# Latent attention beside local attention on one core: the second halves of the queries and keys issued at the end of a step, and the side work dealt out anew over the 36 steps

## The chip, the cores and the metric

One Trainium2 chip, one of its cores. The metric is the device time of one launch in microseconds (us), median of several runs. Times of single instructions come from one profiled execution.

## The reference, cut to what matters

The input x has 8 batches of 1024 rows of 256 numbers, all float32. Two blocks follow each other, each with a layer normalisation ahead of it and a residual sum behind it. The change touches the first one alone, latent attention with a shared rotary part:

```python
c_kv = x @ W_kv_down                                   # 256 -> 128
k_rope = rotary(c_kv @ W_k_rope)                       # 32 wide, one for all heads
k, v = c_kv @ W_k_up, c_kv @ W_v_up                    # 16 heads of 16
q, q_rope = x @ W_q, rotary(x @ W_q_rope)
scores = (q . k per head + q_rope . k_rope) / sqrt(48) # causal
x = x + softmax(scores) @ v @ W_o
```

The second block (two layers of windowed attention with a gated MLP) follows on all batches, and is the same before and after.

## The kernel before, in words

The first block is the function `mla` (lines 156 to 650), the second one `local` (from line 658). In `mla` the attention of one batch is cut into 36 units, one a step (`units`, lines 597 to 603). Steps 0 to 25 treat query columns 512 to 1023 (c = 1), first heads 0 to 7 (g = 0 and 1, steps 0 to 12), then heads 8 to 15 (g = 2 and 3, steps 13 to 25). Steps 26 to 35 treat query columns 0 to 511 (c = 0) in the same two parts. The exponential of a score is a product of two: exp of the head's own part, and `er`, exp of the rotary part, which all heads share.

In step s the main loop (lines 613 to 646) writes out, in this order:

- `scores` of unit s (line 444): 8 score products on TensorE (line 455) into two tiles of two PSUM banks each, pool `pscore`, two such tiles in all; then two exponentials on ScalarE (line 463), one a tile, into `pt` (6 buffers).
- the entries "low" of the step (line 624).
- `turned` of unit s-1 (line 467): two products pt times er on VectorE (line 477).
- `values` of unit s-2 (line 479): the products with v on TensorE (line 488); where a head group ends, ScalarE copies the sum (`oaT`, line 496).
- `do(b, step)` (line 638): the other entries of the step.
- `turn_back` and `finished` for head groups that ended one or two steps earlier (lines 500 to 521): on VectorE a transposition, a reciprocal and a product each, then a transposition for every second group, and after the last one a range test of the reciprocals (lines 1794, 1795, 1788).

All this stands in a manual schedule (line 613), so TensorE, VectorE, ScalarE and GpSimd each run their instructions in the order in which they are written.

The side work of a step is a table (lines 544 to 581) of tuples: the step, whose batch it is (-1 the one before, 0 this one, 1 the next, 2 the one after that), a name, its arguments. The names:

- `statistics(n, part)` (line 268): mean and variance of two row tiles on VectorE; with part 1 the power -1/2 and the shift on GpSimd follow (lines 285 to 288).
- `normalise(n, part)` (line 291): before, two row tiles a call on ScalarE (line 299).
- `turn(n, c)` (line 304): four transpositions on TensorE into one bank, copied by ScalarE to `xnT`.
- `down`, `rope_q`, `rope_k`, `query`, `keys`, `value` (lines 323 to 401): projections, through `dense` (line 313), which may be split over two steps; four column quarters of one product are four matmuls (line 201). `rope_q` and `rope_k` are followed by a VectorE product with the rotary tables (lines 335 and 342), the others by a ScalarE copy.
- `query` and `keys` end in `halves` (line 348): ScalarE copies the sum, rounded to fp32r, into the tile `halves` (two buffers). `low` (line 353) then subtracts that copy from the sum in PSUM by one matmul with minus the identity (line 355), copies the rest as the second half (line 356), and the four transfers of `place_q` or `place_k` (lines 370 and 385) are issued on SyncE.
- `rotary(c, kb)` (line 414): the rotary scores of one key block on TensorE, exp on ScalarE into `er` (line 418), on diagonal blocks a mask on GpSimd (line 420).
- `squares` and `reach` (lines 427 to 437): squares of the rotary parts on ScalarE, sums on TensorE, a maximum on VectorE (a range test).
- `out_add(t, i, c)` (line 523): the product with W_o on TensorE, the residual sum on VectorE (line 534), and the store to `x2d` on SyncE (line 535).
- `load`: the next x, on SyncE.

All of them take a PSUM bank from a pool of two (`psum1`), which is free again when the copy or sum has read it. From step `ALONE` on (line 610: one past the last step in which batch 0 of the table has work other than out_add, 16 before) the last batch gives these two banks to a third pair of score banks (lines 616 to 619). Two passes over the table ahead of the main loop (lines 605 to 608) prepare the first batch.

Of the kernel before, what the change touches and what calls it, by code (L numbers as in the profile page):

```python
# [31 lines left out]
AF = mybir.ActivationFunctionType  # L32
# [50 lines left out]
def preln_mla_local_kernel(  # L83
# [27 lines left out]
    nc = tc.nc  # L111
    B = x.shape[0]
# [43 lines left out]
    def mla(ctx: ExitStack, verdict):  # L156
# [101 lines left out]
        class Batch:  # L258
# [32 lines left out]
            def normalise(self, n, part):  # L291
# [5 lines left out]
                xn = self.xn[n]  # L297
                for i in (2 * part, 2 * part + 1):
                    nc.scalar.activation(
                        xn[:, i, :], self.x[:, 4 * n + i, :], AF.Identity, scale=rstd[:, i : i + 1],  # L300
                        bias=shift[:, i : i + 1],
                    )
# [241 lines left out]
        for step, who, *what in (  # L544
            (0, -1, "out_add", 6, 1, 1), (0, 0, "query", 1, 1, 0),
            (1, 0, "query", 1, 1, 1),
            (2, 0, "low"), (2, 0, "value", 2),
            (3, 0, "keys", 1, 0), (3, 1, "statistics", 1, 1),
            (4, 0, "low"), (4, 0, "keys", 1, 1), (4, 1, "normalise", 0, 0),
            (5, 0, "low"), (5, 0, "query", 0, 0, 0), (5, 1, "normalise", 0, 1),  # L550
            (6, 0, "query", 0, 0, 1), (6, 1, "normalise", 1, 0),
            (7, 0, "low"), (7, -1, "out_add", 0, 0), (7, -1, "out_add", 0, 1),
            (8, -1, "out_add", 2, 0), (8, -1, "out_add", 2, 1),
            (9, 0, "value", 3),
            (10, 0, "query", 1, 0, 0), (10, 1, "normalise", 1, 1),
            (11, 0, "query", 1, 0, 1), (11, 1, "turn", 0, 0),
            (12, 0, "low"), (12, 0, "rotary", 0, 0), (12, 1, "turn", 0, 1),
            (13, 0, "rotary", 0, 2), (13, 1, "down", 0, 0),
            (14, 0, "rotary", 0, 3), (14, 1, "down", 0, 1),
            (15, 0, "rotary", 0, 1), (15, 1, "turn", 1, 0),  # L560
            (16, 1, "down", 1, 0), (16, 1, "turn", 1, 1),
            (17, 1, "down", 1, 1), (17, 1, "rope_q", 0, 0, 0),
            (18, 1, "rope_q", 0, 0, 1), (18, 1, "rope_q", 0, 1),
            (19, 1, "rope_q", 1, 0), (19, 1, "rope_k", 0, 0),
            (20, 1, "rope_k", 0, 1), (20, 1, "rope_q", 1, 1), (20, 2, "load"),
            (21, 1, "rope_k", 1), (21, 1, "query", 0, 1, 0, 0),
# [30 lines left out]
        units = []  # L597
# [15 lines left out]
        with tc.manual_schedule(engines={E.PE, E.DVE, E.Activation, E.Pool}):  # L613
            for b in range(B + 1):
                for step in range(len(units) if b < B else 9):
# [23 lines left out]
                    if turning:  # L639
                        bt, e = turning.pop(0)  # L640
                        bt.turn_back(*e)
# [1250 lines left out]
```

## Time and profile before

| | |
|---|---|
| median of 3 runs | 3263.04 us (3262.31 to 3263.51) |
| the profiled execution | 3258.18 us |
| its span, first to last instruction | 3256.5 us |
| granted TensorE clock | 0.994 |
| busy over the span | PE 97%, DVE 81%, ACT 53%, POOL 41% |
| first exponential of the main loop | at 50.37 us |
| first exponential of batches 1 to 7 | 161.43, 275.25, 389.28, 504.01, 618.03, 731.86, 845.62 us |
| so one batch takes | 111.06 (batch 0), then 113.83, 114.03, 114.73, 114.02, 113.83, 113.77 us |

The last exponential of `mla` starts at 945.96 us; the rest of the span, some 2300 us, is the second block. PE is TensorE's matmuls, PEld its weight loads, DVE is VectorE, ACT ScalarE, POOL GpSimd, SP SyncE. Names are those of the program's tiles: sc are scores, pt their exponentials, acc the products with v, psq, psk, psv, psrq, psrk, psR, psc, psn and psx the banks of query, keys, value, rope_q, rope_k, rotary, down, turn and out_add. "place_q(1, 1)" in a name marks the `halves` tile of query m = 1, n = 1.

### The profile page before, as it was taken

The numbers are of one execution on the slowest core, as the hardware profiler recorded it, in microseconds if no ns is written. First come the engines' busy times: TensorE is split into PE (matmuls) and PEld (weight loads), VectorE is DVE, ScalarE is ACT, GpSimd is POOL, SyncE is SP. The second block draws the span as 40 slices with busy tenths as digits, with TensorE's granted clock in tenths as the row PEclk, the third lists the DMA queues.
The fourth block names the chain that finished last, engine by engine and source line by source line (L and its number), as shares of the span: only waits on it lengthen the run. The fifth ranks groups of instructions, "written<-read, shape, count | busy, mean of one in ns | idle before, by whom it ended". The sixth has DMA issues, their size and how long they took to land.

```text
span 3256.5 us, 112852 instructions
## 1 busy us (share of the span) xinstructions
PE 3161.7 (97%) x50274; PEld 1461.0 (45%) x50274; DVE 2650.2 (81%) x3934; ACT 1733.9 (53%) x2183; POOL 1344.1 (41%) x1065
## 2 busy tenths in 40 slices
PE   7999999999987999999999999999999999999998
PEld 2434343443433444444444444445444444444454
DVE  4999999999988788887878877777787878787773
ACT  6888888888852344444444444444444444444441
POOL 1001000000008665565555555555555555555540
PEclk9999999999998999999999999999999999999999
DMA  4133233323333444544444455455545545454431
GB/s 129 44 92 88 53 79 79 76 59 78 83 122 94 114 126 117 137 118 125 126 117 132 120 145 141 125 128 145 138 131 138 131 125 134 132 146 125 117 107 56
DMA packets 389902, 364.22 MB, mean 112 GB/s; under 512 B 158703, under 2 KB 337310, under 8 KB 389278
## 3 DMA queue, kind: packets, MB, share of 16 engines
q1 hardware_dynamic: 387422, 354.51, 40.8%
q8 instruction: 396, 6.49, 0.8%
q10 hardware_dynamic: 1984, 2.41, 0.2%
q14 instruction: 100, 0.82, 0.1%
HBM read 165.96 MB, written 140.51 MB: 94 GB/s over the span
## 4 chain that ended last, share of the span: by engine, by line
PE 84%; DVE 8%; ACT 3%; DMA 2%; issue 1%; SPq 1%; POOL 1%; ACTq 0%; DVEq 0%; POOLq 0%
PE ag L670 18%; PE pair L670 12%; PE psy L670 9%; PE psw L670 7%; PE acc L488 6%; PE pv L670 6%; PE o L1003 6%; PE sc L455 5%; PE pair L962 4%; DVE pt L477 4%; PE s L1011 2%; PE psx L201 1%; PE psR L201 1%; ACT pt L463 1%; PE psq L201 1%
## 5 line engine op out<-in xcount | busy, mean ns | idle before, releaser
L477 DVE TENSOR_TENSOR pt<-pt,er 128x1024 f32<-128x1024 f32 x576 | 671.7, 1220 | 35.2 <-ACT pt L463 35.1
L670 PE MATMUL ag<-d,l 128*32 128x512 f32 x5632 | 640.2, 593 | 1.2 <-DVE xs L1043 0.7
L906 POOL TENSOR_TENSOR t<-t,t 128x1024 f32<-128x1024 f32 x128 | 304.3, 2377 | 796.8 <-DVE t L902 796.8
L463 ACT ACTIVATE pt<-sc 128x1024 f32<-128x1024 f32 x576 | 561.1, 1033 | 115.1 <-PE sc L455 105.1
L968 ACT ACTIVATE pt<-pair 128x1024 f32<-128x1024 f32 (+1 forms) x256 | 235.2, 968 | 537.0 <-PE pair L962 496.4
L670 PE MATMUL pair<-l_qkv,xT 128*32 128x512 f32 x4096 | 468.6, 598 | 3.2 <-DMA xT<-zx 2.5
L126 POOL TENSOR_TENSOR rn<-ss,half 128x16 f32<-128x16 f32 x128 | 373.0, 2914 | 13.9
L488 PE MATMUL acc<-pt,v 128*32 128x512 f32 (+3 forms) x3072 | 344.8, 495 | 11.6 <-DVE pt L477 10.4
L670 PEld LDWEIGHTS ag<-d,l 128*32 128x32 f32 x5632 | 177.8, 110 | 373.8 <-issue 354.3
L897 ACT ACTIVATE sq<-pair 128x1024 f32<-128x1024 f32 x128 | 131.2, 1025 | 349.2 <-issue 300.6
L670 PE MATMUL psy<-l,hid 128*32 128x256 f32 x5120 | 282.1, 379 | 0.0
L670 PEld LDWEIGHTS pair<-l_qkv,xT 128*32 128x32 f32 x4096 | 131.5, 111 | 303.5 <-issue 276.3
L899 DVE TENSOR_TENSOR t<-pair,l_cos 128x1024 f32<-128x1024 f32 x128 | 156.0, 1219 | 121.6 <-ACT sq L897 121.2
L455 PE MATMUL sc<-q,k 32*128 32x512 f32 (+3 forms) x3072 | 245.9, 380 | 4.0 <-ACT pt L463 3.0
L912 POOL TENSOR_TENSOR t<-t,rn 128x1024 f32<-128x1024 f32 x128 | 243.5, 1902 | 10.0
L1003 PEld LDWEIGHTS o<-pt,v 128*32 128x32 f32 x7680 | 215.1, 110 | 68.1 <-issue 51.8
L1135 DVE SCALAR_TENSOR_TENSOR hid<-ag,l_b,ge 128x512 f32<-128x512 f32 x160 | 116.7, 730 | 157.4 <-ACT ge L1134 88.0
L670 PE MATMUL pv<-l_qkv,xT 128*32 128x512 f32 x2048 | 243.7, 592 | 0.0
L420 POOL TENSOR_SCALAR_AFFINE_SELECT er<-er 128x128 f32<-128x128 f32 x64 | 39.0, 609 | 481.3 <-ACT er L418 481.3
L1003 PE MATMUL o<-pt,v 128*32 128x128 f32 x7680 | 234.5, 273 | 3.1 <-POOL pt L970 2.8
L1021 DVE RECIPROCAL rs<-s 128x256 f32<-128x256 f32 x128 | 223.1, 1743 | 15.8 <-PE s L1011 15.7
L670 PE MATMUL psw<-l_o,oT 128*32 128x256 f32 x4096 | 234.7, 381 | 0.7 <-DVE xs L1172 0.7
(326 smaller groups left out, 4589.9 us busy)
## 6 DMA issues: line engine op xcount, KB each, us to landing
z<-turned SPq DMA_DIRECT2D x512, 128.0 KB, 2.4
qkT<-z SPq DMA_DIRECT2D x128, 512.0 KB, 3.4
y<-xs SPq DMA_DIRECT2D x128, 128.0 KB, 3.0
h<-y SPq DMA_DIRECT2D x32, 512.0 KB, 4.6
zx<-turneds SPq DMA_DIRECT2D x120, 128.0 KB, 3.0
xT<-zx SPq DMA_DIRECT2D x240, 64.0 KB, 2.5
zh<-turnedh SPq DMA_DIRECT2D x120, 128.0 KB, 2.4
d<-zh SPq DMA_DIRECT2D x30, 512.0 KB, 3.2
```

Source lines behind the costliest of these rows:

```text
L126: nc.gpsimd.tensor_tensor(out_, in_, half[:, :n], ALU.pow)
L455: nc.tensor.matmul(two[n // 2][:, n % 2, lo : lo + w], k[rows], q[rows, h], start=(h == 1), stop=(h == 0),)
L463: nc.scalar.activation(pt, sc, AF.Exp, scale=SCALE)
L477: nc.vector.tensor_tensor(t, t, er.to_broadcast([P, 1024 // w, w]), ALU.mult)
L488: nc.tensor.matmul(self.acc[g][32 * n : 32 * n + 32, q0 - c * 512 :], self.v[:, kb, h * VW : h * VW + 32], pts[n // 2][:, n % 2, lo : lo + w],
L670: nc.tensor.matmul(out[four], w[:, four], rhs, start=start, stop=stop)
L899: nc.vector.tensor_tensor(t1, qk, A[:, i].unsqueeze(2).to_broadcast([P, 2, HEADS, DH]), ALU.mult)
L906: nc.gpsimd.tensor_tensor(t1, t1, t2, ALU.add)
L912: nc.gpsimd.tensor_tensor(t1, t1, rn.unsqueeze(3).to_broadcast([P, 2, HEADS, DH]), ALU.mult)
L968: nc.scalar.activation(pt[:, :, : n * P], flat[:, :, : n * P], AF.Exp, scale=-1.0)
L1003: nc.tensor.matmul(o[32 * j : 32 * j + 32, g, a, :], vs[m][:, h * DH + a * 32 : h * DH + a * 32 + 32], pts[m][g][:, place(j), off : off + ...
L1021: nc.vector.reciprocal(rs, s)
```

## The change

The table is laid out anew. Each "low" now stands in the step after the one that completes its product, as before, but is issued after the other entries of that step: `do(b, step, low=True)` moves from behind the scores to behind `do(b, step)`, and so behind the products with v. `normalise` treats one row tile a call, in eight steps (3 to 10) in place of two tiles in four (4, 5, 6 and 10). The two statistics of the upper rows move from steps 34 and 3 to 4 and 5, those of the lower rows from 23 and 26 to 24 and 25. `reach` goes from 32 to 30, an out_add from 31 and 32 to 31, two others from 7 and 8 to 6 and 10. keys(1, 1) goes from step 4 to 11; the rotary blocks of c = 0 from 12 to 15 to 13, 14, 16 and 17, which moves ALONE to 18. The one split rope_k and one split query become whole, one rope_q becomes split. After the last batch the loop runs over 11 steps in place of 9, for the later out_add. No product is added or left out.

```diff
--- before.py
+++ after.py
@@ -294,12 +294,10 @@
                     if n == 0:
                         self.xn = []
                     self.xn.append(p1.tile([P, 4, D], F32, tag="xn", name=f"xn{self.b}_{n}", bufs=2))
-                xn = self.xn[n]
-                for i in (2 * part, 2 * part + 1):
-                    nc.scalar.activation(
-                        xn[:, i, :], self.x[:, 4 * n + i, :], AF.Identity, scale=rstd[:, i : i + 1],
-                        bias=shift[:, i : i + 1],
-                    )
+                nc.scalar.activation(
+                    self.xn[n][:, part, :], self.x[:, 4 * n + part, :], AF.Identity, scale=rstd[:, part : part + 1],
+                    bias=shift[:, part : part + 1],
+                )
 
             def turn(self, n, c):
                 if n == c == 0:
@@ -544,39 +542,39 @@
         for step, who, *what in (
             (0, -1, "out_add", 6, 1, 1), (0, 0, "query", 1, 1, 0),
             (1, 0, "query", 1, 1, 1),
-            (2, 0, "low"), (2, 0, "value", 2),
-            (3, 0, "keys", 1, 0), (3, 1, "statistics", 1, 1),
-            (4, 0, "low"), (4, 0, "keys", 1, 1), (4, 1, "normalise", 0, 0),
-            (5, 0, "low"), (5, 0, "query", 0, 0, 0), (5, 1, "normalise", 0, 1),
-            (6, 0, "query", 0, 0, 1), (6, 1, "normalise", 1, 0),
-            (7, 0, "low"), (7, -1, "out_add", 0, 0), (7, -1, "out_add", 0, 1),
-            (8, -1, "out_add", 2, 0), (8, -1, "out_add", 2, 1),
-            (9, 0, "value", 3),
-            (10, 0, "query", 1, 0, 0), (10, 1, "normalise", 1, 1),
-            (11, 0, "query", 1, 0, 1), (11, 1, "turn", 0, 0),
-            (12, 0, "low"), (12, 0, "rotary", 0, 0), (12, 1, "turn", 0, 1),
-            (13, 0, "rotary", 0, 2), (13, 1, "down", 0, 0),
-            (14, 0, "rotary", 0, 3), (14, 1, "down", 0, 1),
-            (15, 0, "rotary", 0, 1), (15, 1, "turn", 1, 0),
-            (16, 1, "down", 1, 0), (16, 1, "turn", 1, 1),
-            (17, 1, "down", 1, 1), (17, 1, "rope_q", 0, 0, 0),
-            (18, 1, "rope_q", 0, 0, 1), (18, 1, "rope_q", 0, 1),
-            (19, 1, "rope_q", 1, 0), (19, 1, "rope_k", 0, 0),
-            (20, 1, "rope_k", 0, 1), (20, 1, "rope_q", 1, 1), (20, 2, "load"),
-            (21, 1, "rope_k", 1), (21, 1, "query", 0, 1, 0, 0),
-            (22, 1, "query", 0, 1, 0, 1), (22, 1, "query", 0, 1, 1), (22, 1, "squares", 0),
-            (23, 1, "low"), (23, 1, "keys", 0, 0), (23, 2, "statistics", 0, 0), (23, 1, "squares", 1),
-            (24, 1, "low"), (24, 1, "value", 0),
-            (25, 1, "value", 1),
-            (26, 1, "keys", 0, 1), (26, 2, "statistics", 0, 1),
-            (27, 1, "low"), (27, 1, "rotary", 1, 0),
-            (28, 1, "rotary", 1, 1),
-            (29, 1, "rotary", 1, 2), (29, 1, "rotary", 1, 7),
-            (30, 1, "rotary", 1, 3),
-            (31, 1, "rotary", 1, 6), (31, 0, "out_add", 4, 0),
-            (32, 0, "out_add", 4, 1), (32, 1, "reach"),
-            (33, 1, "rotary", 1, 4),
-            (34, 1, "rotary", 1, 5), (34, 2, "statistics", 1, 0),
+            (2, 0, "value", 2), (2, 0, "low"),
+            (3, 0, "keys", 1, 0), (3, 1, "normalise", 0, 0),
+            (4, 0, "query", 0, 0, 0), (4, 0, "low"), (4, 1, "normalise", 0, 1), (4, 1, "statistics", 1, 0),
+            (5, 0, "query", 0, 0, 1), (5, 1, "normalise", 0, 2), (5, 1, "statistics", 1, 1),
+            (6, -1, "out_add", 0, 0), (6, -1, "out_add", 0, 1), (6, 0, "low"), (6, 1, "normalise", 0, 3),
+            (7, 0, "query", 1, 0, 0), (7, 1, "normalise", 1, 0),
+            (8, 0, "query", 1, 0, 1), (8, 1, "normalise", 1, 1),
+            (9, 0, "value", 3), (9, 0, "low"), (9, 1, "normalise", 1, 2),
+            (10, -1, "out_add", 2, 0), (10, -1, "out_add", 2, 1), (10, 1, "normalise", 1, 3),
+            (11, 0, "keys", 1, 1),
+            (12, 1, "turn", 0, 0), (12, 0, "low"),
+            (13, 0, "rotary", 0, 2), (13, 1, "turn", 0, 1),
+            (14, 1, "down", 0, 0), (14, 0, "rotary", 0, 3),
+            (15, 1, "down", 0, 1), (15, 1, "turn", 1, 0),
+            (16, 0, "rotary", 0, 0), (16, 1, "turn", 1, 1),
+            (17, 1, "down", 1, 0), (17, 0, "rotary", 0, 1),
+            (18, 1, "down", 1, 1), (18, 1, "rope_q", 0, 0, 0),
+            (19, 1, "rope_q", 0, 0, 1), (19, 1, "rope_q", 0, 1),
+            (20, 1, "rope_k", 0), (20, 1, "rope_q", 1, 0, 0), (20, 2, "load"),
+            (21, 1, "rope_q", 1, 0, 1), (21, 1, "rope_q", 1, 1),
+            (22, 1, "rope_k", 1), (22, 1, "query", 0, 1, 0),
+            (23, 1, "query", 0, 1, 1), (23, 1, "squares", 0),
+            (24, 1, "value", 0), (24, 1, "low"), (24, 1, "squares", 1), (24, 2, "statistics", 0, 0),
+            (25, 1, "keys", 0, 0), (25, 2, "statistics", 0, 1),
+            (26, 1, "value", 1), (26, 1, "low"),
+            (27, 1, "keys", 0, 1), (27, 1, "rotary", 1, 7),
+            (28, 1, "rotary", 1, 0), (28, 1, "low"),
+            (29, 1, "rotary", 1, 1), (29, 1, "rotary", 1, 6),
+            (30, 1, "reach"),
+            (31, 0, "out_add", 4, 0), (31, 0, "out_add", 4, 1),
+            (32, 1, "rotary", 1, 3),
+            (33, 1, "rotary", 1, 2),
+            (34, 1, "rotary", 1, 4), (34, 1, "rotary", 1, 5),
             (35, 0, "out_add", 6, 0), (35, 0, "out_add", 6, 1, 0),
         ):
             at(step, who, *what)
@@ -612,7 +610,7 @@
         line, done, turning = [], [], []
         with tc.manual_schedule(engines={E.PE, E.DVE, E.Activation, E.Pool}):
             for b in range(B + 1):
-                for step in range(len(units) if b < B else 9):
+                for step in range(len(units) if b < B else 11):
                     if b == B - 1 and step == ALONE:
                         banks.close()
                         third = banks.enter_context(tc.tile_pool(name="pscore2", bufs=1, space=PSUM))
@@ -621,7 +619,6 @@
                         if step == 0:
                             batches[b].start()
                         line.append((batches[b], units[step], batches[b].scores(step, units[step])))
-                    do(b, step, low=True)
                     if len(line) > 1 or b == B:
                         for bt, unit, pts in line[-2 : -1] if b < B else line[-1:] if step == 0 else []:
                             bt.turned(unit, pts)
@@ -636,6 +633,7 @@
                         for act, args in held[2:]:
                             act(*args)
                     do(b, step)
+                    do(b, step, low=True)
                     if turning:
                         bt, e = turning.pop(0)
                         bt.turn_back(*e)
```

## The prediction

> **What bounds the kernel now.** I read the page first, then the steady batch from 275.25 to 389.28 us in four views: busy time by stage, the chain of waits, the timeline of TensorE, the groups by form on each engine.
>
> ```profile
> PE 3161.7 (97%) x50274; PEld 1461.0 (45%) x50274; DVE 2650.2 (81%) x3934; ACT 1733.9 (53%) x2183; POOL 1344.1 (41%) x1065
> ```
> ```profile
> 275.25:389.28 114.03, 111.31 (x1290) 45.65 (x1292) 105.66 (x131) 96.64 (x128) 9.62 (x14) 1.00 0.30 75
> ```
>
> In the stage that changes, the columns are PE, PEld, DVE, ACT and POOL busy: PE 111.3 of 114.0, DVE 105.7, ACT 96.6. Three engines are nearly full, so small local overloads decide. The chain shows an undisturbed step, and three kinds of disturbed ones:
>
> ```profile
> 335.46 0.66 PE sc L455 x5
> 336.13 1.00 PE acc L488 x8
> 337.13 0.86 PE psrq L201 x8
> 337.99 0.43 PE psrk L201 x8
> 338.42 0.67 PE sc L455 x6
> ...
> 284.22 0.47 SPq L370
> ...
> 286.05 5.09 DMA q<-alves_place_q(1, 1)_3282
> 291.23 0.59 ACT alves_place_k(1, 1)_3410 L79
> 291.87 0.49 PE psk L355
> ...
> 351.54 1.10 ACT sq L430
> 352.64 1.83 ACT pt L463 x2
> 354.52 0.79 PE sc L455 x12
> ...
> 382.44 0.63 DVE onat L504
> 383.10 0.26 DVE rs L506
> 383.38 0.42 DVE onat L510
> 383.81 2.38 DVE pt L477 x2
> 386.23 0.84 PE acc L488 x10
> ```
>
> The first five lines price a step on TensorE: scores 0.67, values 0.99, a 512-column product 0.86, a half of one 0.43. The next four show keys(1, 1) of step 4 waiting for the tile `halves` whose transfers, started in step 3, land 7.0 us after the copy (284.22 to 291.2); low and the values stand behind it. Then ScalarE sets the pace (a square, then the exponentials of step 24). Last, VectorE: the closing of a head group and a pt pair, while the values of step 35 wait.
>
> **What TensorE itself needs.** 36 x (0.67 + 0.99) = 59.8; 26 projections (8 query, 4 each of keys, value, down, rope_q, 2 rope_k) x 0.86 = 22.4; rotary 9 x 512 columns, 7.7; out_add 8 x 0.86 = 6.9; low 8 x 0.43 = 3.4; turns 4 x 0.59 = 2.4; reach 0.9. Sum 103.5. So 114.0 holds 10.5 us of waits. From the starts of the score groups in the timeline of TensorE, interval less own work, I find them in: steps 34, 35 and 0 (VectorE): 1.3 + 1.4 + 0.8 = 3.5. Steps 2, 4, 5, 7 (low, halves): 0.5 + 0.5 + 1.8 + 0.6 = 3.4. Steps 23 to 29 (ScalarE): 2.4. Steps 10 to 12 and 16: 0.9; the rest 0.3.
> VectorE needs 72 products at 1.13 (2.27 a pair) = 81.7, 8 closings at 1.37 (382.44 to 383.81), 4 transpositions at 0.62, a range test 0.75, statistics 3.9, 4 rotary products, 4 residual sums and reach at 0.61: 105.4. That is the floor under any order.
>
> [...]111.3 busy, 103.5 of work. [...]the square at 351.54 holds back exponentials whose scores are ready. [...]here 5.09 us for the last of four transfers of 256 KB, and I use that.
>
> **The change part by part, for a steady batch.** No product is added or removed, so 103.5 and 105.4 stay; normalise splits a call, not an instruction (8 x 0.61 us either way).
>
> *Low at the end of a step.* Before, low waits for a copy that ScalarE does behind both exponentials of the step before, so TensorE loses its lead over ScalarE in each low step. After, 1.85 us or more of values and projection (0.99 + 0.86) lie between, and the copy is long done. Its second copy comes due about 0.1 us after low, ahead of the next exponentials, which can't start until the scores have run 0.67: it takes 0.48 of pace there and is hidden. If ScalarE is late, it costs up to 0.48 a low.
>
> *keys(1, 1) at step 11.* Its `halves` buffer then belongs to query(0, 0), sent off at step 7: 4 steps, over 11 us, against a landing of 7. The 1.8 of step 5 goes. query(0, 0) in step 5 takes the buffer of query(1, 1), sent at the start of step 3: 8.2 us at the least, slack 1.2. keys(0, 1) in step 27 takes that of query(0, 1), sent early in step 25: 8.1 us, slack 1.1.
>
> *Steps 1 to 11 on ScalarE.* Work a step is 1.83 for the exponentials and 0.48 to 0.50 for each copy or normalise: 2.8 in steps 1 to 6, 3.3 in step 9, against TensorE's 2.52 to 3.8. Its lag reaches 0.2, 0.2 and 0.6, each gone a step later; exponentials and scores chained give 2.58 in the shortest steps. I take 0.4 in place of 3.4 (steps 2 to 7), VectorE apart.
>
> *Steps 12 to 15.* Step 13 has oaT, rotary and turn copies on ScalarE, 3.1 against TensorE's 2.67: 0.6 lost in steps 13 and 14. Before, this stretch lost about as much.
>
> *Steps 23 to 29.* Query copy and square in step 23 (1.83 + 0.48 + 0.96 = 3.27 against 2.53), value, square and low's copy in step 24 (3.75 against 2.95), less in step 25 (2.3 against 2.6): the lag passes on as 0.1, 0.3 and 1.2 us, and 0.1 in step 27. Sum 1.7, before 2.4.
>
> *VectorE, steps 30 to 35 and 0.* reach and out_add leave step 32 for 30 and 31, statistics leave 34. I follow the start of each pt pair behind the start of its scores: start(s) = start(s-1) + 2.27 + extra work; the values two steps on need it 2.41 later. Checked on before: pair 32 starts at 380.09, 5.5 behind its scores, and its values are due 6.6 behind; 5.5 + 2.4 - 6.6 = 1.3, as found. After, pairs 31 to 34 start 4.0, 4.3, 5.3 and 5.6 behind: the values of 32 wait 0.8, those of 33 0.4, those of 34 nothing. Sum 1.3, before 3.5.
>
> *VectorE, steps 1 to 6.* Here the statistics go to. Two closings (1.37), transposition and range test (1.38), 0.87 and 1.08 in steps 1 to 5 stand over pairs of 2.27, against steps of 2.6 to 2.95: pairs 2, 3 and 4 start 5.1, 5.8 and 6.1 behind, and steps 3 to 6 wait 0.2, 0.9, 0.7 and 0.5. Sum 2.4, new in the open: before, step 5's low stall and the ScalarE waits hid most of it. The out_add of step 6 (TensorE 3.8) ends it.
>
> *GpSimd and SyncE.* The power behind statistics(1, 1) (1.45 + 0.21 + 0.71 us of POOL) ends some 0.3 us into step 7; normalise(1, 0) is due 2.6 into it. If it were late, the exponentials of step 8 would queue behind it. On SyncE the x2d store of step 6 now stands ahead of place_q(0, 0) and waits for a VectorE sum: under 1 us, and its q is read from step 26 on. The store of step 10 has nothing behind it before step 12. Both free.
>
> *Sum.* After: 0.4 + 0.6 + 1.7 + 1.3 + 2.4, and 0.8 for split score groups and 2.58-us steps = 7.2. Gain 10.5 - 7.2 = 3.3 a batch, period 110.7.
>
> *Ends.* Batch 0 has no closings or out_add in steps 0 to 10, so none of the 2.4; I take 4.5. Batches 1 to 6: 6 x 3.3 = 19.8. In the last batch VectorE runs without a pause from about step 14 (48.2 of 50 us busy from 900 to 950), so only the first steps count: 1. The third score pair comes at step 18, not 16; VectorE is late by then, and the l_cos product that waits for weights (7.70 us from their release) moves behind pair 19 with it: nothing, between -1 and +2. The preparation keeps its order but for keys after value: nothing, -1 to +1. Sum 25.3, which takes the profiled 3258.2 to 3233; that execution lies 4.9 below the median, so I set it against the median: 3263.0 - 25 = 3238. Each local wait may be off by a third: +-8.
>
> **Rivals.** (A) The stalls only move: with VectorE's statistics in steps 4 and 5 its backlog runs on to step 10 and ScalarE's 24 to 26 costs 3. For it: VectorE's floor is 105.4 of 110.7. Against: the two wide out_add steps. Gain 1 a batch: 3255. (B) All stalls but VectorE's floor go, since the waits overlap: period near 107, 7 x 7 = 49: 3214. For it: waits of two engines in one step count once. Against: the loads of steps 24 and 25 and of 1 to 5 are uneven by the listing itself. (C) Slower: keys(0, 1) in step 27 waits for the transfers of query(0, 1). Low's copy there sits behind a square, so they leave 2 us into step 25. They must land within 8.1 us; the trace has 7.0 for the like. Every us beyond stops the exponentials behind the copy, 7 times. From 8.1 + 3.6 = 11.7 it decides; at 13 it gives 3263 - 25 + 34 = 3272. Against: no other large transfer runs in steps 24 to 27. (D) The late low changes nothing since its copies stand ahead of the exponentials either way: 3263.
>
> **How the numbers follow.** Forecast (3228 to 3248) 0.62; A 0.14; B 0.12; C 0.07; D 0.05. 0.2% is 6.5 us, about what a measurement of this kernel can tell from no change. Faster by that: forecast, B and half of A and a little more, 0.83; within: half of A, D, 0.10; slower 0.07. The range reaches towards A and B: 3220 to 3254.
>
> **What would show it.** Period of batches 1 to 6 near 110.7. The wait of keys(1, 1) for DMA gone; no wait of L355 over 0.3. In steps 34 and 35 the values wait 1.3 for DVE in all, in steps 3 to 6 2.4. Step 25 near 3.7 us for ScalarE. DVE busy unchanged at 105.7. Wrong if the period is above 113 or below 108.5, or if ACT waits for a DMA in step 27.

## The result and the profile after

The changed kernel takes 3240.81 us (median of 6 runs, 3237.17 to 3242.15) against 3262.75 us for the kernel before on the same chip (6 runs, 3262.31 to 3263.73): a ratio of 0.9931, 95% interval 0.9919 to 0.9944, or 21.9 us less. The profiled execution took 3241.02 us, its span is 3239.2.

| | before | after | difference | predicted |
|---|---|---|---|---|
| first exponential (end of the preparation) | 50.37 | 47.20 | -3.2 | 0 |
| batch 0 | 111.06 | 107.96 | -3.1 | -4.5 |
| batches 1 to 6, together | 684.2 | 668.2 | -16.0 | -19.8 |
| one of them | 113.77 to 114.73 | 111.36 to 111.40 | -2.7 | -3.3 |
| last batch, first exponential to last pair | 100.34 | 100.94 | +0.6 | -1 |
| last pair of exponentials | 945.96 | 924.33 | -21.6 | -25.3 |

The last row is the start of the last pair; the very last exponential starts 0.9 us later in both. What comes after that pair is nearly all the second block, the same code in both: 2310.5 us in the one profile and 2314.9 in the other, and 2310.5 to 2320.1 over all profiles of this study. The medians, over six executions each, depend less on this accident.

The page's busy times after, and three of its groups (columns: busy time, mean ns of one, idle time of the engine just before them and what ended it):

```profile
PE 3159.7 (98%) x50210; PEld 1462.9 (45%) x50210; DVE 2648.5 (82%) x3934; ACT 1734.7 (54%) x2183; POOL 1355.6 (42%) x1065
...
L475 DVE TENSOR_TENSOR pt<-pt,er 128x1024 f32<-128x1024 f32 x576 | 672.5, 1219 | 13.4 <-ACT pt L461 13.1
...
L461 ACT ACTIVATE pt<-sc 128x1024 f32<-128x1024 f32 x576 | 561.8, 1035 | 92.7 <-PE sc L453 83.3
...
L486 PE MATMUL acc<-pt,v 128*32 128x512 f32 (+3 forms) x3072 | 342.3, 496 | 6.4 <-DVE pt L475 6.3
```

TensorE, VectorE and ScalarE work as long as before within 2 us of the whole span; the idle time ahead of the pt products fell from 35.2 to 13.4 us, that ahead of the exponentials from 115.1 to 92.7. Lines of the changed kernel stand two lower than those of the kernel before: L475 is its L477. The steady batch, busy time by stage (columns PE, PEld, DVE, ACT, POOL busy, clock):

```profile
266.51:377.88 111.37, 110.77 (x1284) 45.88 (x1287) 105.34 (x131) 96.66 (x128) 11.43 (x14) 1.00 0.30 77
```

The chain of waits through steps 3 to 6 of that batch, where before keys(1, 1) stood waiting for its transfers:

```profile
277.01 0.91 PE sc L453 x5
277.92 1.44 PE acc L486 x6
279.36 0.01 PE psq L201 x2
279.37 0.42 PE acc L486 x2
279.79 0.86 PE psq L201 x6
280.65 0.44 PE psk L353
...
281.75 1.25 PE acc L486 x6
...
283.16 0.27 PE acc L486 x2
...
286.37 1.92 PE psx L201 x29
```

No DMA is left in it. But the values of step 4 take 1.44 + 0.42 where undisturbed ones take 0.99: the eight matmuls are started piecemeal, as VectorE finishes one pt tile after the other. This is how a wait looks that doesn't show as idle time, since the matmuls that are under way count as busy. Per step of that batch, interval between score groups less TensorE's own work, the waits that I find are: steps 4 to 6, mostly for VectorE, 2.4 (1.1 + 0.7 + 0.6; of the 1.1 some 0.2 lie in the scores, 0.91 in place of 0.67), 34 and 35 for VectorE 1.3, 23 to 29 for ScalarE 2.1, 12 to 15 0.8, the rest 1.3: in all 7.9, predicted 7.2.

A last pair of rows, from the waits view from 150 to 950 us, first of the kernel before, then of the changed one (sum, times, longest):

```profile
DVE pt L477 <- ACT pt L463: 22.4, 28, 1.5
DVE x L534 <- PE psx L201: 20.9, 21, 2.5
...
DVE rq L335 <- PE psrq L201: 6.4, 6, 1.1
```
```profile
DVE x L532 <- PE psx L201: 19.5, 14, 2.3
DVE rq L333 <- PE psrq L201: 11.1, 6, 1.9
...
DVE pt L475 <- ACT pt L461: 3.6, 12, 1.4
```

VectorE waited for exponentials 28 times before, now 12 times, and 18.8 us less in all, while its waits for the rope_q product grew by 4.7. The same window in us isn't the same stretch of work in the two kernels; in batches 1 to 6 alone the first row goes from 21.8 to 3.6 us. The prediction had not read these rows; kernel 12 below comes back to them.

### The profile page after: what moved, and what is told of

The parts are those of the page before. It is cut to its first block, busy times and chain, and to the rows that moved or that the text cites. A ratio compares the mean times of both kernels' runs of the same rounds, so it can differ in the third digit from the quotient of the medians.

```text
span 3239.2 us, 112711 instructions
## 1 busy us (share of the span) xinstructions
PE 3159.7 (98%) x50210; PEld 1462.9 (45%) x50210; DVE 2648.5 (82%) x3934; ACT 1734.7 (54%) x2183; POOL 1355.6 (42%) x1065
## 4 chain that ended last, share of the span: by engine, by line
PE 91%; DVE 4%; DMA 2%; ACT 1%; POOL 1%; SPq 1%; issue 1%; DVEq 0%; ACTq 0%
PE ag L668 18%; PE pair L668 13%; PE psy L668 10%; PE acc L486 9%; PE psw L668 7%; PE sc L453 6%; PE pv L668 6%; PE o L1001 6%; PE pair L960 5%; PE psR L201 2%; PE psx L201 2%; PE psq L201 2%; PE s L1009 2%; PE psc L201 1%; PE psrq L201 1%; PE psv L201 1%
## 5 line engine op out<-in xcount | busy, mean ns | idle before, releaser
L475 DVE TENSOR_TENSOR pt<-pt,er 128x1024 f32<-128x1024 f32 x576 | 672.5, 1219 | 13.4 <-ACT pt L461 13.1
L461 ACT ACTIVATE pt<-sc 128x1024 f32<-128x1024 f32 x576 | 561.8, 1035 | 92.7 <-PE sc L453 83.3
L418 POOL TENSOR_SCALAR_AFFINE_SELECT er<-er 128x128 f32<-128x128 f32 x64 | 51.1, 802 | 481.1 <-ACT er L416 481.1
```

Source lines behind the costliest of these rows:

```text
L461: nc.scalar.activation(pt, sc, AF.Exp, scale=SCALE)
L475: nc.vector.tensor_tensor(t, t, er.to_broadcast([P, 1024 // w, w]), ALU.mult)
```

## The experiments

All are set against the kernel before, on the same chip as the runs beside them. "Period" is the time of one of batches 1 to 6 in the profile; "VectorE idle" is the sum of all gaps above 0.1 us between VectorE's instructions in batch 2. A step is timed here from the start of its first exponential to that of the next step's, as a mean over batches 1 to 6 where no batch is named. VectorE's busy time in that batch is 105.2 to 105.9 in all of them, and its smaller gaps add up to 0.8, so a longer period is longer idle time of VectorE by bookkeeping; that alone says nothing about the cause, but it shows where the time lies.

| kernel | median us | ratio to before, 95% | period | VectorE idle |
|---|---|---|---|---|
| before | 3262.75 | | 113.77 to 114.73 | 7.60 |
| after | 3240.81 | 0.9931 (0.9919 to 0.9944) | 111.37 | 5.26 |
| 1 after, low early | 3237.98 | 0.992 (0.9903 to 0.9936) | 111.26 | 5.16 |
| 2 before, low late | 3269.76 | 1.0027 (1.0016 to 1.0037) | 115.14 to 116.04 | 8.88 |
| 3 before, keys(1, 1) later | 3272.82 | 1.0034 (1.0022 to 1.0046) | 116.04 to 116.30 | 9.56 |
| 4 after, upper statistics back | 3246.88 | 0.9953 (0.9936 to 0.997) | 112.70 | 6.41 |
| 5 before, rotary moved | 3267.59 | 1.001 (1.0003 to 1.0017) | 114.40 to 115.84 | 8.09 |
| 6 after, statistics away | 3237.64 | 0.9923 (0.9907 to 0.994) | 110.75 | 4.59 |
| 7 after, squares earlier | 3232.83 | 0.9906 (0.989 to 0.9923) | 110.42 | 4.44 |
| 8 both of 6 and 7 | 3229.52 | 0.9896 (0.9879 to 0.9912) | 109.82 | 3.77 |
| 9 before, upper statistics moved | 3258.6 | 0.9987 (0.998 to 0.9993) | 113.09 to 115.01 | 6.93 |
| 10 before, 3 and 9 together | 3257.48 | 0.9981 (0.9974 to 0.9988) | 113.63 | 7.10 |
| 11 as 8, range test later | 3227.06 | 0.9888 (0.9872 to 0.9905) | 109.35 | 3.28 |
| 12 steps 0 to 17 of 10, rest of after | 3252.6 | 0.9969 (0.9958 to 0.998) | 113.04 | 6.69 |

### 1. Low early in the new table

```diff
                         line.append((batches[b], units[step], batches[b].scores(step, units[step])))
+                    do(b, step, low=True)
...
                     do(b, step)
-                    do(b, step, low=True)
```

> The changed kernel with one part undone: the low of a step stands again behind its scores, ahead of the values and the projection. Theory (the late low keeps TensorE's lead over ScalarE): eight lows a batch lose 0.3 to 0.5 us each, so the period of batches 1 to 6 goes from 111.4 to about 114 and the time rises by some 20 us. Rival (the place of low is worth nothing, the new table alone makes the gain): period 111.4 to 111.7, time within 3 us of the changed kernel.

The theory fell: the period is 111.26 against 111.37. In the single steps something is to be seen: step 2, which has a low, takes 3.26 instead of 2.95, step 28 3.21 instead of 2.90. But steps 4 to 6 together take 10.63 instead of 11.36 (2.99, 4.02 and 3.62 in place of 3.72, 3.59 and 4.05). TensorE loses 0.3 us as was said, at two of the eight lows, and waits 0.7 less in these three steps, where VectorE is behind. In the new table the place of low is worth nothing.

### 2. Low late in the old table

```diff
-                self.pending = ps, t, then, args
+                self.pending = getattr(self, "pending", []) + [(ps, t, then, args)]
...
-                ps, t, then, args = self.pending
+                ps, t, then, args = self.pending.pop(0)
...
-                    do(b, step, low=True)
                     if len(line) > 1 or b == B:
...
                     do(b, step)
+                    do(b, step, low=True)
```

> The kernel before with the late low alone; its table stays, and the pending halves become a queue, since two products are pending at times. Theory: the 1.6 us of steps 2, 4 and 7 go and some of the 2.4 of steps 23 to 29, while keys(1, 1) still waits for its transfers (1.8 us): period from 114.0 to about 112, gain some 15 us. Rival (late low changes nothing by itself): period 113.8 or more, gain under 3 us.

Neither: the old table is slower with the late low, by 1.5 us a batch. The timeline of ScalarE shows why. First the kernel before, then this one (start, duration, instruction, count, idle time before it and what ended it):

```profile
281.73 1.99 ACT L463 ACTIVATE pt<-sc 128x1024 f32<-128x1024 f32 x2
283.55 0.65 ACT L79 CAST alves_place_q(1, 1)_3282<-psq 128x512 fp32r<-128x512 f32 x1
...
291.23 0.59 ACT L79 CAST alves_place_k(1, 1)_3410<-psk 128x512 fp32r<-128x512 f32 x1 [1.28 <-DMA q<-alves_place_q(1, 1)_3282]
```
```profile
283.56 1.98 ACT L463 ACTIVATE pt<-sc 128x1024 f32<-128x1024 f32 x2
...
285.93 0.59 ACT L79 CAST alves_place_q(1, 1)_3282<-psq 128x512 fp32r<-128x512 f32 x1
...
293.67 0.59 ACT L79 CAST alves_place_k(1, 1)_3402<-psk 128x512 fp32r<-128x512 f32 x1 [2.60 <-DMA q<-alves_place_q(1, 1)_3282]
```

The second half of query(1, 1) is copied 1.8 us behind the exponentials' start before, 2.4 behind it here, half a us later, as the value's copy of that step now stands ahead of it, and its transfers leave later. The copy of keys(1, 1) waits 2.60 us instead of 1.28, since on ScalarE it also comes sooner: the second copy of keys(1, 0), which stood ahead of it, now stands behind it and waits with it. Step 4 takes 6.41 in place of 5.19. In this table a late low costs mostly because it makes transfers late that are waited for; 0.4 more is lost in step 12.

### 3. keys(1, 1) later in the old table

```diff
-            (4, 0, "low"), (4, 0, "keys", 1, 1), (4, 1, "normalise", 0, 0),
-            (5, 0, "low"), (5, 0, "query", 0, 0, 0), (5, 1, "normalise", 0, 1),
+            (4, 0, "low"), (4, 1, "normalise", 0, 0),
+            (5, 0, "query", 0, 0, 0), (5, 1, "normalise", 0, 1),
...
-            (9, 0, "value", 3),
-            (10, 0, "query", 1, 0, 0), (10, 1, "normalise", 1, 1),
+            (9, 0, "value", 3), (9, 0, "keys", 1, 1),
+            (10, 0, "low"), (10, 0, "query", 1, 0, 0), (10, 1, "normalise", 1, 1),
```

> The kernel before with keys(1, 1) alone moved from step 4 to 9 and its low from 5 to 10. Theory: the wait of 1.8 us for the transfers goes and low costs 0.4 in step 10 instead of step 5: period from 114.0 to about 112.4, gain some 12 us, no L355 wait ended by a DMA. Rival (the stall only moves, to ScalarE or VectorE): period 113.7 or more.

Again neither. The wait for the transfers is gone, step 4 takes 3.28 in place of 5.19; but step 5 takes 6.16 in place of 3.27. TensorE in step 5, its timeline, and then its busy time and clock in four stretches (the clock is the number ahead of the last two):

```profile
288.95 0.94 PE L455 MATMUL sc<-q,k 32*128 32x512 f32 x8
291.55 2.20 PE L488 MATMUL acc<-pt,v 128*32 128x512 f32 x6 [1.66 <-DVE pt L477]
```
```profile
286.00:291.00 5.00, 3.89 (x32) 1.43 (x25) 4.90 (x12) 4.93 (x8) 1.76 (x3) 1.00 0.93 230
...
292.00:295.00 3.00, 3.00 (x14) 0.68 (x12) 3.00 (x4) 1.36 (x3) 0.00 (x0) 0.51 0.02 7
295.00:296.00 1.00, 1.00 (x8) 0.12 (x8) 1.00 (x2) 0.00 (x0) 0.00 (x0) 0.77 0.00 0
296.00:300.00 4.00, 4.00 (x37) 1.42 (x41) 3.46 (x4) 3.34 (x5) 0.00 (x0) 1.00 0.00 0
```

TensorE arrives earlier at values whose pt VectorE has not done: VectorE is busy 4.90 of the 5.00 us from 286 to 291 and all of the time from 292 to 296, with the closings, the statistics, the range test. So the wait moves by a step and is VectorE's. Behind this wait of 1.66 us the clock falls to half for 3.41 us (0.51 from 292 to 295 us), and so in each of batches 1 to 6. TensorE is busy throughout those us, so this costs some 1.7 us, an estimate: half of 3.41. Without it the period would be about 114.4 by this estimate, still no less than before.

### 4. The upper statistics back

```diff
-            (3, 0, "keys", 1, 0), (3, 1, "normalise", 0, 0),
-            (4, 0, "query", 0, 0, 0), (4, 0, "low"), (4, 1, "normalise", 0, 1), (4, 1, "statistics", 1, 0),
-            (5, 0, "query", 0, 0, 1), (5, 1, "normalise", 0, 2), (5, 1, "statistics", 1, 1),
+            (3, 0, "keys", 1, 0), (3, 1, "statistics", 1, 1), (3, 1, "normalise", 0, 0),
+            (4, 0, "query", 0, 0, 0), (4, 0, "low"), (4, 1, "normalise", 0, 1),
+            (5, 0, "query", 0, 0, 1), (5, 1, "normalise", 0, 2),
...
-            (34, 1, "rotary", 1, 4), (34, 1, "rotary", 1, 5),
+            (34, 1, "rotary", 1, 4), (34, 1, "rotary", 1, 5), (34, 2, "statistics", 1, 0),
```

> The changed kernel with the two statistics of the upper rows back in steps 34 and 3 of the table, from 4 and 5. Theory (VectorE's backlog from step 32 to step 6 is one queue, and the place of the statistics in it decides only where TensorE waits): the waits of steps 34, 35 and 0 grow from 1.3 to about 3, those of 4 to 6 fall from 2.4 to about 0.7; period 111.4 within 0.5. Rival (moving the statistics out of step 34 is what makes the gain): period above 113.

Between the two, nearer the rival: 112.70, so the place of the upper statistics is worth 1.3 of the 2.7 us. Step 0 takes 3.71 in place of 2.96 and step 5 4.67 in place of 3.59, each with the pt pairs behind one of the statistics; step 6 is 0.6 shorter. The two aren't one queue in which only the place of the wait changes: with nothing left to do behind the pairs of step 5, VectorE comes to the residual sum of step 6 early and idles 0.88 us for its product, which it didn't in the changed kernel. Statistics in steps 4 and 5 fill that time.

```profile
290.59 0.69 DVE L532 TENSOR_TENSOR x<-psx,x 128x512 f32<-128x512 f32 x1 [0.88 <-PE psx L201]
```

### 5. The rotary blocks moved alone

```diff
-            (12, 0, "low"), (12, 0, "rotary", 0, 0), (12, 1, "turn", 0, 1),
+            (12, 0, "low"), (12, 1, "turn", 0, 1),
...
-            (15, 0, "rotary", 0, 1), (15, 1, "turn", 1, 0),
-            (16, 1, "down", 1, 0), (16, 1, "turn", 1, 1),
-            (17, 1, "down", 1, 1), (17, 1, "rope_q", 0, 0, 0),
+            (15, 1, "turn", 1, 0),
+            (16, 0, "rotary", 0, 0), (16, 1, "down", 1, 0), (16, 1, "turn", 1, 1),
+            (17, 0, "rotary", 0, 1), (17, 1, "down", 1, 1), (17, 1, "rope_q", 0, 0, 0),
```

> The kernel before with one piece of the new table alone: the rotary blocks (0, 0) and (0, 1) go from steps 12 and 15 to 16 and 17. New theory, after the first four runs (a batch takes VectorE's 105.7 us plus VectorE's idle time; the kernel before has 7.6 us of idle, of it 2.05 in steps 12 and 13, where TensorE's and ScalarE's steps are longer than VectorE's): most of the 2.05 goes, period from 114.0 to about 112.4, gain some 11 us. Rival (the idle time only moves to step 16 to 18): period 113.7 or more.

The rival held, and a batch is even some 0.5 us longer (the longest, 115.84, has 3.41 us of half clock besides). Step 12 is 1.06 shorter, steps 16 and 17 are 1.0 and 0.8 longer, and VectorE waits there instead:

```profile
319.47 2.36 DVE L477 TENSOR_TENSOR pt<-pt,er 128x1024 f32<-128x1024 f32 x2 [0.45 <-ACT pt L463]
...
337.08 0.69 DVE L335 TENSOR_TENSOR rq<-psrq,tab 128x512 f32<-128x512 f32 x1 [2.62 <-PE psrq L201]
```

Before, the two waits were 1.47 and 1.08. Step 16 now holds a rotary block, a down and a turn beside scores and values, 0.67 + 0.99 + 0.86 + 0.86 + 0.59 = 3.97 of TensorE's own work. The new table moves down and rope_q on by a step as well; these moves together were not tried apart from the rest of it.

### 6. Statistics away from steps 4 and 5

```diff
-            (4, 0, "query", 0, 0, 0), (4, 0, "low"), (4, 1, "normalise", 0, 1), (4, 1, "statistics", 1, 0),
-            (5, 0, "query", 0, 0, 1), (5, 1, "normalise", 0, 2), (5, 1, "statistics", 1, 1),
+            (4, 0, "query", 0, 0, 0), (4, 0, "low"), (4, 1, "normalise", 0, 1),
+            (5, 0, "query", 0, 0, 1), (5, 1, "normalise", 0, 2),
...
-            (12, 1, "turn", 0, 0), (12, 0, "low"),
+            (12, 1, "turn", 0, 0), (12, 0, "low"), (12, 2, "load"),
...
-            (19, 1, "rope_q", 0, 0, 1), (19, 1, "rope_q", 0, 1),
-            (20, 1, "rope_k", 0), (20, 1, "rope_q", 1, 0, 0), (20, 2, "load"),
+            (19, 2, "statistics", 0, 0), (19, 2, "statistics", 0, 1), (19, 1, "rope_q", 0, 0, 1), (19, 1, "rope_q", 0, 1),
+            (20, 1, "rope_k", 0), (20, 1, "rope_q", 1, 0, 0),
...
-            (24, 1, "value", 0), (24, 1, "low"), (24, 1, "squares", 1), (24, 2, "statistics", 0, 0),
-            (25, 1, "keys", 0, 0), (25, 2, "statistics", 0, 1),
+            (24, 1, "value", 0), (24, 1, "low"), (24, 1, "squares", 1), (24, 2, "statistics", 1, 0),
+            (25, 1, "keys", 0, 0), (25, 2, "statistics", 1, 1),
```

> The changed kernel with its load in step 12 (before 20), the statistics of the lower rows in step 19 ahead of the rotary product there, and those of the upper rows in 24 and 25, so that steps 4 and 5 have none. New theory (VectorE's idle time decides): 1.95 us of statistics fill the 1.86 us in which VectorE waits in step 19, period from 111.4 to about 109.5, gain some 13 us against the changed kernel. The sum of the waits in the prediction says the same, 2.4 less: 109.0. Rival (TensorE and ScalarE set the pace of steps 18 to 22, and the work only moves): period 111 or more.

Better, but by 0.6 us and not by 1.9 or 2.4: neither the theory nor the sum of the waits had the size, and the rival missed too. The 1.86 us of step 19 are filled, at no cost to TensorE (steps 18 to 22 are unchanged). Steps 4 and 5 take 3.73 and 3.59 as before; only step 6 is shorter, by 0.6. The statistics in steps 4 and 5 weren't what TensorE waited for there. And VectorE, rid of them, idles again ahead of the sum of step 6:

```profile
286.17 0.69 DVE L532 TENSOR_TENSOR x<-psx,x 128x512 f32<-128x512 f32 x1 [0.88 <-PE psx L201]
...
298.43 0.69 DVE L532 TENSOR_TENSOR x<-psx,x 128x512 f32<-128x512 f32 x1 [2.10 <-PE psx L201]
```

### 7. Squares a step earlier

```diff
-            (22, 1, "rope_k", 1), (22, 1, "query", 0, 1, 0),
-            (23, 1, "query", 0, 1, 1), (23, 1, "squares", 0),
-            (24, 1, "value", 0), (24, 1, "low"), (24, 1, "squares", 1), (24, 2, "statistics", 0, 0),
+            (22, 1, "rope_k", 1), (22, 1, "query", 0, 1, 0), (22, 1, "squares", 0),
+            (23, 1, "query", 0, 1, 1), (23, 1, "squares", 1),
+            (24, 1, "value", 0), (24, 1, "low"), (24, 2, "statistics", 0, 0),
```

> The changed kernel with the squares in steps 22 and 23, from 23 and 24. By the sum of the waits: ScalarE's lag of 1.5 us in steps 24 to 26 falls to about 0.2, period 110.1. New theory (VectorE's idle time decides): at most the 0.20, 0.28 and 0.67 us in which VectorE waits in steps 26, 30 and 31 can go, period 110.3 to 110.6. Rival (VectorE is behind there anyway and sets the pace): 111.2 or more.

Period 110.42, in the range of the VectorE theory; the sum of the waits had said 110.1. Step 24 falls from 3.70 to 2.75, and no other step changes by more than 0.02. The stretch in the changed kernel that this removes is, in its chain of waits,

```profile
343.38 1.00 PE acc L486 x16
344.38 0.06 PE psk L201
344.44 1.85 ACT pt L461 x2
346.29 0.04 issue
346.34 0.72 PE sc L453 x5
```

two exponentials behind a square, with TensorE standing. The wait that the prediction had found for ScalarE in this place was a real one: taken away, it stayed away, though not all of it went.

### 8. The two together

> The edits of the two runs before it (statistics away from steps 4 and 5, squares in 22 and 23) together, on the changed kernel. If both act by themselves, the gains add up: period about 108.3, time some 21 us under the changed kernel. Rival (both take from one slack): no better than the better of the two.

Period 109.82: 0.62 and 0.95 expected from the single runs, 1.55 found. The gains add; both were only smaller than expected.

### 9 and 10. The upper statistics in the old table, without and with keys(1, 1)

```diff
-            (3, 0, "keys", 1, 0), (3, 1, "statistics", 1, 1),
-            (4, 0, "low"), (4, 0, "keys", 1, 1), (4, 1, "normalise", 0, 0),
-            (5, 0, "low"), (5, 0, "query", 0, 0, 0), (5, 1, "normalise", 0, 1),
-            (6, 0, "query", 0, 0, 1), (6, 1, "normalise", 1, 0),
+            (3, 0, "keys", 1, 0),
+            (4, 0, "low"), (4, 0, "keys", 1, 1), (4, 1, "normalise", 0, 0), (4, 1, "statistics", 1, 0),
+            (5, 0, "low"), (5, 0, "query", 0, 0, 0), (5, 1, "normalise", 0, 1), (5, 1, "statistics", 1, 1),
+            (6, 0, "query", 0, 0, 1),
...
-            (8, -1, "out_add", 2, 0), (8, -1, "out_add", 2, 1),
+            (8, -1, "out_add", 2, 0), (8, -1, "out_add", 2, 1), (8, 1, "normalise", 1, 0),
...
-            (34, 1, "rotary", 1, 5), (34, 2, "statistics", 1, 0),
+            (34, 1, "rotary", 1, 5),
```

> The kernel before with its statistics of the upper rows alone moved, from steps 34 and 3 to 4 and 5 (normalise(1, 0) follows from 6 to 8). Theory (in steps 3 to 5 TensorE waits for two things at once, keys(1, 1)'s transfers and VectorE's backlog; one removed leaves the other): steps 34 to 0 gain 0.75, but keys(1, 1) still waits, period 113.0 to 113.6. Rival (the place of the statistics by itself is worth the 1.3 us that undoing it cost in the new table): period 112.7 or less.

> The kernel before with both pieces: keys(1, 1) to step 9 and the statistics of the upper rows to 4 and 5. keys(1, 1) alone made a batch 2.2 us longer, 1.7 of it a window of TensorE's clock at half rate behind a wait of over 1.6 us for VectorE. Theory (two waits that cover each other): with both gone no wait is that long, the clock stays full, period 112.0 or less. Rival (the pieces add up): 2.2 more and 1.3 less than before, period about 114.9.

The statistics alone give 113.09 to 113.37 (115.01 in one batch, in which the copy of keys(1, 1) waited 2.5 us for the transfers and TensorE 2.3 us for that copy): the 0.75 us of step 0, as the theory had it. Kernel 10 adds the edit of experiment 3 to this. The half clock of kernel 3 doesn't come in any of its batches, as expected: TensorE's longest wait for pt from 150 to 900 us is 0.6 us, 1.7 in kernel 3, and the mean clock of the profile 0.993 against 0.99. But its period is 113.63, neither 112.0 or less nor the rival's 114.9, and its time is that of kernel 9. Steps 4 and 5 together take 6.95 us, against 8.3 to 8.5 in the other batches of kernel 9. Of this difference 1.29 (0.86 and 0.43) is just the work of keys(1, 1) and its low, which turns up in steps 9 and 10; and steps 6 and 7 are 0.8 longer, as VectorE's backlog is now what TensorE meets there. So the wait of keys(1, 1) for its transfers covered a wait for VectorE, and its removal is worth nothing in this table, with the statistics moved or not.

### 11. The range test in step 10

```diff
-                if (c, g) == (0, 3):
-                    verdict(self.rs.rearrange("p c g b -> p (c g b)"), f"a{self.b}")
+            def bounds(self):
+                verdict(self.rs.rearrange("p c g b -> p (c g b)"), f"a{self.b}")
...
-            (10, -1, "out_add", 2, 0), (10, -1, "out_add", 2, 1), (10, 1, "normalise", 1, 3),
+            (10, -1, "bounds"), (10, -1, "out_add", 2, 0), (10, -1, "out_add", 2, 1), (10, 1, "normalise", 1, 3),
```

> The changed kernel with statistics away from steps 4 and 5, squares in 22 and 23, and the range test of the reciprocals (0.75 us of VectorE, until now in step 3) in step 10, ahead of the residual sum there. Theory (VectorE's backlog sets steps 3 to 6, and it waits 2.1 us for the out_add product of step 10): the test fills part of that wait, period from 109.83 to about 109.1, time some 5 us less than without this last piece. Rival (TensorE's own work sets these steps): period 109.7 or more.

The theory held: step 5 falls from 3.59 to 2.91, step 6 gives 0.22 back, the period is 109.35 (0.47 less; 0.7 had been expected). The test, 0.75 us of VectorE, now stands in the wait for the sum of step 10, which is that much shorter:

```profile
294.30 0.29 DVE L1787 TENSOR_REDUCE good<-oka 128x1 f32<-128x128 f32 x1
295.90 0.69 DVE L533 TENSOR_TENSOR x<-psx,x 128x512 f32<-128x512 f32 x1 [1.32 <-PE psx L201]
```

This is the fastest kernel of the study by its median, 3227.06 us. Its interval overlaps that of kernel 8, so in time the two aren't told apart; the periods of the profiles are.

### 12. Half of each table

Steps 0 to 17 are those of kernel 10 (without rope_q in step 17), steps 18 to 35 those of the change (without down in step 18); low stays early.

```diff
-            (17, 1, "down", 1, 1), (17, 1, "rope_q", 0, 0, 0),
-            (18, 1, "rope_q", 0, 0, 1), (18, 1, "rope_q", 0, 1),
...
+            (17, 1, "down", 1, 1),
+            (18, 1, "rope_q", 0, 0, 0),
+            (19, 1, "rope_q", 0, 0, 1), (19, 1, "rope_q", 0, 1),
...
```

> Steps 0 to 17 of the run before the last (the old table with keys(1, 1) and the statistics of the upper rows moved, low early), steps 18 to 35 of the new table. Period of the one 113.6, of the new table 111.4: which half holds the 2.3 us? Theory (VectorE's idle time decides: 4.1 us of it in steps 7 to 13 of the old half, none there but 2.1 in step 10 of the new): the first half holds it, period 113.0 to 113.6. Rival (the evening out of steps 22 to 35 holds it): period 111.4 to 112.0.

Period 113.04, as the theory had it. From kernel 10 to this one the second half of the table gives 0.6 us, from this one to the changed kernel the first half gives 1.7. In its waits from 150 to 950 us the row that was 22.4 before and is 3.6 after still stands:

```profile
DVE pt L477 <- ACT pt L463: 23.1, 29, 1.5
```

VectorE idles ahead of the pairs that it does in steps 11, 12 and 13, while TensorE has 3.54 us of own work in step 12 alone (0.67 + 0.99 + 0.43 low + 0.86 rotary + 0.59 turn):

```profile
309.90 2.36 DVE L477 TENSOR_TENSOR pt<-pt,er 128x1024 f32<-128x1024 f32 x2 [0.95 <-ACT pt L463]
312.86 2.36 DVE L477 TENSOR_TENSOR pt<-pt,er 128x1024 f32<-128x1024 f32 x2 [0.60 <-ACT pt L463]
316.69 2.36 DVE L477 TENSOR_TENSOR pt<-pt,er 128x1024 f32<-128x1024 f32 x2 [1.47 <-ACT pt L463]
```

The new table has no such step there: 8 to 15 take 2.65 to 3.32, and of VectorE's waits in steps 7 to 13 only the 2.10 us ahead of the sum of step 10 are left.

The waits of TensorE put the same 1.7 us elsewhere: 1.3 of it in steps 2 to 7 (3.9 there in kernel 12, 2.7 in the changed one), 0.3 in steps 23 to 29 and 0.2 in steps 10 to 12, of which the other steps take 0.1 back. In steps 2 to 6, where VectorE is behind, kernel 12 has 12.6 us of TensorE's own work and the new table 14.75, with an out_add in step 6 instead of 7 and half of a query in each of steps 4 and 5 instead of 5 and 6; so TensorE comes later to the pairs that it would wait for. Both accounts add up, and no run here tells which of the two is the cause.

## Why the prediction came out

The time was foreseen within 3 us of the median, and the 2.7 us a batch within 0.6. The waits by step added up to 7.9 us where 7.2 were foreseen. But the reasons were partly others, and that the time came so close is in part luck: the batches gave less than foreseen, the preparation, set at nothing, gave more. (Two sums of the prediction are 0.1 too high as written: 0.2 + 0.9 + 0.7 + 0.5 is 2.3, 0.8 + 0.4 is 1.2.)

*Where the 2.7 us come from.* Read from before to after by kernels 10 and 12: the upper statistics and keys(1, 1) give 0.4, the layout of steps 18 to 35 0.6, that of steps 0 to 17 with the late low 1.7. The order matters, though: undone in the new table, the statistics alone are worth 1.3 (kernel 4), in the old one some 0.7 (kernel 9). Which of the edits in steps 0 to 17 makes how much of the 1.7 wasn't taken apart further; kernel 1 says that the late low isn't it, kernel 5 that the rotary blocks aren't by themselves. What remains is how the queries, the out_add products and the rotary, turn and down work are spread, and that was argued from kernel 12 only.

*"Low at the end of a step"*: this step failed. That TensorE loses its lead at an early low is true and can be seen (0.3 us in step 2). What it loses there it need not wait for later, because VectorE is behind in these steps; 0.1 us of a batch and no more depends on it, and that the other way round. Rival D had this edit's worth in the new table, though not its reason, since the place of low does shift single steps by 0.3; and it was wrong on the whole.

*"keys(1, 1) at step 11: the 1.8 of step 5 goes"*: the wait went, as told, and no time with it (kernels 3 and 10). The prediction took waits step by step and added them up; two that cover each other were counted as if they stood alone. It had named this for VectorE's backlog ("before, step 5's low stall and the ScalarE waits hid most of it") and booked it as a new cost of 2.4 beside a gain of 1.8, so the sum came out nearly right: a mistake in the one term was made good by the other.

*"VectorE, steps 30 to 35 and 0"*: right in size, 1.3 left of 3.5.

*"VectorE, steps 1 to 6: here the statistics go to"*: the size was right, 2.4, the share of the statistics wasn't. Without them 1.8 of it remains (kernel 6), and the range test is 0.5 of that (kernel 11). What is early in the queue delays the pairs; the statistics, which stand behind them and ahead of a sum that waits for its product, cost 0.6 for their 1.95 us.

*"Steps 23 to 29 on ScalarE"*: 2.1 for 1.7, and 0.95 of it goes with the squares (kernel 7). This was the term whose mechanism and size held best.

*"Steps 12 to 15 ... before, this stretch lost about as much"*: TensorE's waits there are 0.8 for 0.6, and were 0.4 before. The other engine wasn't looked at: VectorE, whose 105.3 us of work are more than TensorE's 103.5, idled 2.05 us in steps 12 and 13 of the kernel before and doesn't in the changed one. Whether that time was lost isn't shown: kernel 5 took 1.0 us of it away, and VectorE's wait for the rope_q product grew by 1.5.

*Ends.* Batch 0 gave 3.1 for 4.5, the last batch took 0.6 more: l_cos waits 0.7 us longer for its weights, which are released two steps later than before. That this makes the 0.6 was read from the chain and not tried. There is a rival to it: the last batch of the changed kernel has 3.41 us of half clock (0.50) at 888.54 us, that of the kernel before none. Kernel 4 has none either and takes as long there as the changed kernel within 0.1 us, which speaks for the wait and doesn't settle it. The preparation, set at nothing, gave 3.2: in the profile of before it holds 3.41 us of half clock (0.50), from 43.30 us, which cost up to 1.7 (half of 3.41, an estimate); the first exponential of the kernels with the old table, or its first half, comes at 48.4 to 52.1 us, of those with the new one at 45.9 to 47.2. So a part of it is the change's own, by a cause that was not looked for, and what was off in the other terms was made good by it. This is the luck in the number.

*Rivals.* A (stalls only move) describes what single edits of this change do in the old table, kernels 2, 3 and 5. B would have needed periods near 107; 109.35 was reached with three more edits. C, the wait for transfers in step 27, doesn't occur: no copy of halves waits for a DMA in the changed kernel.

## What to carry to other kernels

Where two engines are nearly full, list the waits of both by step before adding any: a wait of TensorE in a stretch where VectorE has a backlog isn't worth what it lasts (kernels 3 and 10; in kernel 3 step 4 fell by 1.9 us and step 5 grew by 2.9, of which some 1.7 by the half clock), and idle time of VectorE in a stretch where TensorE is full can't be had by moving one piece of TensorE's work out of it, when that piece fills another step (kernel 5: step 12 1.06 us shorter, steps 16 and 17 1.0 and 0.8 longer). Work that only the second engine does (statistics, a range test) goes where that engine stands waiting, ahead of the instruction that waits, and behind everything that others wait for (kernel 11: 0.47 us a batch for the range test). And a single edit of a schedule may cost by itself what it gains with the others: three of four parts tried alone in the old table made it slower.

## What the hardware showed that had not been expected

In all six steady batches of kernel 3 a wait of TensorE for one pt tile, 1.65 to 1.67 us long, was followed within 0.8 us by 3.41 us at half clock. In batch 2 the wait of 1.66 us ends at 291.55, and the clock is 1.00 from 286 to 292 us, 0.51 from 292 to 295, 0.77 from 295 to 296 and 1.00 after that. TensorE has work throughout there (3.00 of 3.00 us busy from 292 to 295), so half clock costs some 1.7 us beside the wait itself, an estimate from half of the 3.41 us.

The length of a single wait doesn't decide it. In step 4 of batch 3 of the kernel before, TensorE waits 1.67 us, up to 406.60 us, and in that of its other batches 0.7 to 1.2 us, and the clock stays at 1.00 from 46.71 to 945 us. In the last batch of the changed kernel two waits of 1.18 and 1.21 us, which end at 886.35 and 888.29 with 0.74 us of matmuls between them, have 3.41 us at a clock of 0.50 behind them, from 888.54 us. What sorts these cases is not shown here: no run moved a wait to try it.
